# Seven products of halves for eight in the projections of an attention layer, and bv added to the residual

## The chip, the cores and the metric

The kernel runs on one core of a Trainium2 chip. The metric is device time in microseconds (us), the median of several runs; all runs told of here are in the fast state, that is, within 1.5% of the fastest run of the same kernel. In this kernel TensorE does the matrix products and writes them to PSUM, a memory in banks; VectorE, ScalarE and GpSimd do the rest between PSUM and SBUF, the memory of the operands, GpSimd on SBUF alone. The operand of a product that stays in TensorE while the other streams past is brought by an instruction of its own, the weight load. The granted clock is the share of TensorE's full speed that the profile shows. All data is float32.

In the profile's lines PE is TensorE, PEld its weight loads, DVE VectorE, ACT ScalarE, POOL GpSimd and SP SyncE, which starts transfers; L324 is a line of the kernel, `sc` are the scores, `pav` is the weighted sum, and `...` marks lines left out.

## The reference, cut to what matters

```python
# x: (128 batches, 128 nodes, 512 features); adj: (128, 128); H, HD = 8, 64
h = relu(layernorm(x))
A = einsum('od,bdn->bon', adj, h)                 # layer 0: W1 = W2 = adj, so that
x = x + max over n of relu(A + b)                 # its pairwise form comes down to this
h = relu(layernorm(x))                            # layer 1: adding a constant per row changes no layernorm
q, k, v = (h @ W + b for W, b in (Wq,bq), (Wk,bk), (Wv,bv))
scores = q k^T / sqrt(64), masked where adj == 0
x = x + softmax(scores) @ v                       # per head
```

The kernel therefore normalises once and uses the same h for both layers. Three 512 x 512 projections of 128 x 128 rows are most of the arithmetic.

## The kernel before

Batches go in 32 groups of four (G = 4, so T = 512 columns in a group). The loop is software-pipelined by hand: each group has four slots, one per batch. In a slot TensorE does a batch's scores, a piece of the next group's projections, and the batch's weighted sum (`finish`). Behind the loop the sums of the exponentials are tested (tile `ok`), and a general form of the kernel stands by for the case that one is out of range.

```python
def slice_q(g):                      # slice_k is the same with ScalarE; slice_v swaps the operands
    QT[g] = proj.tile([P, NC, T], F32, name="qT")
    for f in range(NC):
        pq = ps_mm.tile([P, 512], F32, name="mm")
        for c in range(NC):
            nc.tensor.matmul(pq, W["q"][:, c, f * P : (f + 1) * P], HT[g][:, c, :],
                             start=(c == 0), stop=(c == NC - 1))
        nc.vector.tensor_scalar(QT[g][:, f, :], pq, bq_sb[:, f : f + 1], HD ** -0.5,
                                op0=ALU.add, op1=ALU.mult)
# ... slice_h: four transposes and one adjacency product per batch, hT by ScalarE, maxima by VectorE
slices = (slice_h, slice_q, slice_k, slice_v)
# ... scores: 8 matmuls, two exps on ScalarE, two mask multiplications on VectorE
# ... finish: 8 matmuls (pav), reciprocal, o, y = X + c + o, store
for g in (0, 1):                     # the start
    for n in [norm(g, i) for i in range(G)]:
        norm_end(*n)
    if g == 0:
        for s in slices:
            s(0)
for g in range(NG):                  # the loop
    for i in range(G):
        # ...
        w = scores(g, i)
        n = norm(g + 2, i) if g + 2 < NG else None
        if g + 1 < NG:
            slices[i](g + 1)
        if n is not None:
            norm_end(*n)
        finish(g, i, w)
```

## Time and profile before

| | before |
|---|---|
| median | 1913.45 us (1913.2 to 1915.55, 4 runs) |
| TensorE busy | 1885.2 us, 7939 instructions |
| VectorE / ScalarE / GpSimd busy | 822.2 / 385.3 / 88.1 us |
| mean granted TensorE clock | 0.991 |
| one group in mid-run | 58.46 us |
| one projection of a group | 13.83 us |

The group's period is the distance of two starts of the q projection, 1011.92 us (shown in the prediction) and

```profile
1070.38 14.00 PE L272 MATMUL mm<-hT,wq_sb 128*128 128x512 f32 x32
```

The page is read from the chain that ended last and not from the busy shares: a busy TensorE is only the bound if the chain never leaves it.

### The profile page before, as it was taken

The page shows a single profiled execution, that of the slowest core. Times are in us where ns is not written, and L with a number is a line of the kernel's source. Part 1 is how long each engine was busy: PE and PEld are TensorE (multiplying, and loading weights), DVE is VectorE, ACT ScalarE, POOL GpSimd, SP SyncE. Part 2 cuts the span into 40 slices and gives each one's busy share as a digit, 9 for nine tenths or more (in the row PEclk, how much of TensorE's full clock was granted, in tenths as well). Part 3 has the DMA queues.
Part 4 walks back from the last instruction along what each step waited for, and adds up shares of the span by engine and source line. Part 5 has one row for each costly group of instructions (what it writes and reads, how often), then busy time and mean ns, then how long its engine had stood idle before and what let it go on. Part 6 is the DMA issues. An engine that isn't in the chain of part 4 may idle for free.

```text
span 1913.6 us, 19386 instructions
## 1 busy us (share of the span) xinstructions
PE 1885.2 (99%) x7939; PEld 1052.8 (55%) x7939; DVE 822.2 (43%) x1574; ACT 385.3 (20%) x641; POOL 88.1 (5%) x142
## 2 busy tenths in 40 slices
PE   7999999999999999999999999999999999999997
PEld 3455555555555555555555555555555555555555
DVE  2544344443445443444434454434444344544333
ACT  1222121221212221211212122212112121222110
POOL 1000000000000000000000000000000000000000
PEclk9999999999999999999999999999999999999996
DMA  4011011110111110111101111101111011110000
GB/s 161 11 39 39 17 39 45 39 45 12 44 39 45 39 39 17 40 44 39 45 11 45 39 44 39 39 17 41 42 39 45 11 45 39 45 39 17 17 20 31
DMA packets 37836, 71.87 MB, mean 38 GB/s; under 512 B 3249, under 2 KB 3377, under 8 KB 37745
## 3 DMA queue, kind: packets, MB, share of 16 engines
q1 hardware_dynamic: 35840, 67.12, 9.8%
q10 hardware_dynamic: 1728, 3.21, 0.5%
q8 instruction: 64, 1.05, 0.2%
q0 software_dynamic: 176, 0.27, 0.1%
q14 instruction: 28, 0.22, 0.0%
HBM read 37.03 MB, written 33.55 MB: 37 GB/s over the span
## 4 chain that ended last, share of the span: by engine, by line
PE 98%; DVE 1%; DMA 0%; ACT 0%; issue 0%; POOL 0%; SPq 0%; DVEq 0%
PE mm L272 23%; PE mm L298 23%; PE mm L286 23%; PE pav L332 12%; PE sc L315 7%; PE mm L263 6%; PE mm L256 3%; DMA xg<-in_x_dram 0%; DVE w L325 0%; DVE st L234 0%; DVE hn L240 0%; ACT w L323 0%; DVE y L344 0%; DVE o L340 0%; DVE mv L235 0%
## 5 line engine op out<-in xcount | busy, mean ns | idle before, releaser
L272 PE MATMUL mm<-hT,wq_sb 128*128 128x512 f32 x1024 | 448.0, 595 | 0.0
L298 PE MATMUL mm<-wv_sb,hT 128*128 128x512 f32 x1024 | 447.9, 595 | 0.0
L286 PE MATMUL mm<-hT,wk_sb 128*128 128x512 f32 x1024 | 447.9, 595 | 0.0
L323 ACT ACTIVATE w<-sc 128x512 f32<-128x512 f32 x256 | 138.9, 594 | 907.5 <-PE sc L315 907.5
L272 PEld LDWEIGHTS mm<-hT,wq_sb 128*128 128x128 f32 x1024 | 191.9, 190 | 234.0 <-issue 229.3
L286 PEld LDWEIGHTS mm<-hT,wk_sb 128*128 128x128 f32 x1024 | 192.0, 190 | 233.8 <-issue 222.9
L298 PEld LDWEIGHTS mm<-wv_sb,hT 128*128 128x128 f32 x1024 | 192.0, 190 | 233.8 <-issue 230.1
L332 PEld LDWEIGHTS pav<-v,w 128*128 128x128 f32 x2048 | 254.2, 195 | 66.7 <-issue 66.3
L332 PE MATMUL pav<-v,w 128*128 128x65 f32 x2048 | 249.0, 276 | 6.2 <-DVE w L325 6.1
L338 DVE RECIPROCAL RS<-pav 128x8 f32<-128x8 f32 x128 | 26.6, 208 | 480.6 <-PE pav L332 480.6
L302 DVE TENSOR_TENSOR v<-mm,bv_sb 128x512 f32<-128x512 f32 x128 | 88.5, 692 | 288.1 <-PE mm L298 288.1
L276 DVE TENSOR_SCALAR qT<-mm,bq_sb 128x512 f32<-128x512 f32 x128 | 96.1, 751 | 268.6 <-PE mm L272 268.6
L325 DVE TENSOR_TENSOR w<-w,live 128x512 f32<-128x512 f32 x256 | 165.6, 689 | 5.6 <-ACT w L323 4.5
L239 POOL TENSOR_TENSOR rstd<-ve,mhalf 128x1 f32<-128x1 f32 x128 | 84.4, 659 | 1720.2 <-DVE ve L237 1720.2
L290 ACT ACTIVATE kT<-mm,bk_sb 128x512 f32<-128x512 f32 x128 | 87.9, 687 | 359.8 <-PE mm L286 359.8
L315 PE MATMUL sc<-qT,kT 64*128 64x128 f32 x2048 | 151.5, 288 | 0.0
L263 PE MATMUL mm<-hn,adjT 128*128 128x512 f32 x256 | 133.5, 603 | 4.7 <-DVE adjT L225 4.3
L315 PEld LDWEIGHTS sc<-qT,kT 64*128 64x128 f32 x2048 | 126.7, 190 | 9.5 <-issue 0.8
L247 ACT ACTIVATE hn<-hn,rstd 128x512 f32<-128x512 f32 x128 | 92.1, 720 | 187.0 <-POOL rstd L239 187.0
L344 DVE SCALAR_TENSOR_TENSOR y<-xg,c,o 128x512 f32<-128x512 f32 x128 | 96.2, 752 | 4.5
L256 PEld LDWEIGHTS mm<-ident,hn 128*128 128x128 f32 x512 | 60.2, 143 | 65.9 <-issue 27.4
L234 DVE BATCH_NORM_STATS2 st<-xg 128x6 f32<-128x512 f32 x128 | 87.9, 687 | 7.3 <-DMA xg<-in_x_dram 7.3
(33 smaller groups left out, 487.5 us busy)
## 6 DMA issues: line engine op xcount, KB each, us to landing
xg<-in_x_dram SPq DMA_DIRECT2D x64, 512.0 KB, 4.6
out_dram<-y SPq DMA_DIRECT2D x128, 256.0 KB, 2.0
wq_sb<-in_L_gnn_Wq_dram ACTq DMA_DIRECT2D x1, 1024.0 KB, 11.0
wk_sb<-in_L_gnn_Wk_dram ACTq DMA_DIRECT2D x1, 1024.0 KB, 15.8
wv_sb<-in_L_gnn_Wv_dram ACTq DMA_DIRECT2D x1, 1024.0 KB, 19.7
bv_sb<-in_L_gnn_bv_dram POOLq DMA_DIRECT2D x1, 256.0 KB, 8.0
adj_sb<-in_adj_dram ACTq DMA_DIRECT2D x1, 64.0 KB, 2.4
b_sb<-in_L_gnn_b_dram POOLq DMA_DIRECT2D x1, 0.5 KB, 6.4
```

The lines of the kernel that those rows point to most:

```text
L247: nc.scalar.activation(HN[g][:, i, :], HN[g][:, i, :], AF.Copy, scale=rstd)
L256: nc.tensor.transpose(ph[:, c * D : (c + 1) * D], HN[g][:, i, c * P : (c + 1) * P], ident)
L263: nc.tensor.matmul(pa, adjT, HN[g][:, i, :], start=True, stop=True)
L272: nc.tensor.matmul(pq, W["q"][:, c, f * P : (f + 1) * P], HT[g][:, c, :], start=(c == 0), stop=(c == NC - 1),)
L276: nc.vector.tensor_scalar(QT[g][:, f, :], pq, bq_sb[:, f : f + 1], HD ** -0.5, op0=ALU.add, op1=ALU.mult,)
L286: nc.tensor.matmul(pk, W["k"][:, c, f * P : (f + 1) * P], HT[g][:, c, :], start=(c == 0), stop=(c == NC - 1),)
L298: nc.tensor.matmul(pv, HT[g][:, c, i * D : (i + 1) * D], W["v"][:, c, :], start=(c == 0), stop=(c == NC - 1),)
L315: nc.tensor.matmul(psc[:, j, f, :], KT[g][r, f, i * D : (i + 1) * D], QT[g][r, f, i * D : (i + 1) * D], start=True, stop=True,)
L323: nc.scalar.activation(w[:, j], psc[:, j], AF.Exp)
L325: nc.vector.tensor_tensor(w[:, j], w[:, j], live_h, op=ALU.mult)
L332: nc.tensor.matmul(pav[:, h // 4, (h % 4) * HE : (h % 4 + 1) * HE], w[:, h % 2, h // 2, :], V[g % 2][:, i, h, :], start=True, stop=True,)
L344: nc.vector.scalar_tensor_tensor(y, X[g][:, i, :], C[g][:, i : i + 1], o.rearrange("p k h d -> p (k h d)"), op0=ALU.add, op1=ALU.add,)
```

## The change

The intent is to spend fewer columns of TensorE's time on the projections, with one level of Strassen's method in the form of Winograd. Both operands are cut into halves along both axes; seven products of halves and some sums give what eight products gave. The sums of the weights are made once; those of hT, four per group, are VectorE's. Sums of products are made in two ways: a product is accumulated into a PSUM bank that holds another one, or VectorE adds a copy while it empties the bank. Since a bias would have to pass through these sums, bv is added to the residual X instead, on GpSimd; the weights of a softmax add up to one, so bv would pass through the weighted sum unchanged. The q scale moves into the exp. The transposes of a group move one slot ahead, as its sums are needed earlier. The tiles of `work`, the masked scores among them, get two buffers for three, and hn one for two. The cut shortens some lines; comments stand for the bodies of p1 to p7.

```diff
+            t1, t2, t3, t4 = (hs[:, k] for k in range(4))      # end of slice_h
+            nc.vector.tensor_sub(t1, b12, b11)
+            nc.vector.tensor_sub(t2, b22, t1)
+            nc.vector.tensor_sub(t3, b22, b12)
+            nc.vector.tensor_sub(t4, b21, t2)
+            def mm(self, bank, a, b, first=False):              # one product of halves
+                for r in range(2):
+                    for c in range(2):
+                        nc.tensor.matmul(
+                            bank[:, r, :], a[:, c, r * P : (r + 1) * P], b[:, c, :],
+                            start=first and r == 0 and c == 0, stop=r == 1 and c == 1, ...)
+            def p1(self): # bank a = a11 b11; ScalarE copies it out with each half's bias: pf[0], pf[1]
+            def p6(self): # bank b = s2 t2;   VectorE: u2 = b + pf[0]
+            def p2(self): # bank a += a12 b21; ScalarE: block (0, 0)
+            def p5(self): # bank c = s1 t1
+            def p7(self): # bank b += s3 t3;  VectorE: u3 = b + pf[1], block (1, 1) = c + u3
+            def p4(self): # bank b += a22 t4; VectorE: block (1, 0) = b + pf[1]
+            def p3(self): # bank c += s4 b22; VectorE: block (0, 1) = c + u2
+            return (                                            # the four slots
+                (q.p1, q.p6, q.p2, q.p5, q.p7, k.p1),
+                (q.p4, q.p3, k.p6, k.p2, k.p5, k.p7),
+                (v.p1, k.p4, k.p3, v.p6, v.p2, v.p5, v.p7),
+                (v.p4, v.p3),
+            )
+            nc.gpsimd.tensor_tensor(X[g][:, i, :], X[g][:, i, :], bv_sb, op=ALU.add)   # norm_end
-                    for s in slices:
-                        s(0)
+                slice_h(g)
+                if g == 0:
+                    weight_sums(nc.vector, "q")
+                    weight_sums(nc.gpsimd, "k")
+                    weight_sums(nc.gpsimd, "v")
+                    for part in products(0): ...
```

More of the change, by code (lines that the diff above doesn't have):

```diff
@@ L169, in tile_adj_preln_d2 @@
     T = G * D
+    HT2 = T // 2
     const = ctx.enter_context(tc.tile_pool(name="const", bufs=1))
@@ L173, in tile_adj_preln_d2 @@
     W = {n: const.tile([P, NC, N], F32, name=f"w{n}_sb") for n in "qkv"}
+    WS = {n: const.tile([P, 4, 2, N // 2], F32, name=f"s{n}_sb") for n in "qkv"}
     b0_sb = const.tile([P, 1], F32, name="b0_sb")
@@ L189, in fast @@
         proj = ctx.enter_context(tc.tile_pool(name="proj", bufs=2))
-        work = ctx.enter_context(tc.tile_pool(name="work", bufs=3))
+        work = ctx.enter_context(tc.tile_pool(name="work", bufs=2))
+        tmp = ctx.enter_context(tc.tile_pool(name="tmp", bufs=2))
         stat = ctx.enter_context(tc.tile_pool(name="stat", bufs=8))
@@ L194, in fast @@
         ps_av = ctx.enter_context(tc.tile_pool(name="ps_av", bufs=1, space=PSUM))
-        X, HN, HT, QT, KT, C, AMAX = {}, {}, {}, {}, {}, {}, {}
+        X, HN, HT, HB, QT, KT, C, AMAX, WA = {}, {}, {}, {}, {}, {}, {}, {}, {}
         def load(g):
@@ L230, in norm @@
             if i == 0:
-                HN[g] = proj.tile([P, G, N], F32, name="hn")
+                HN[g] = proj.tile([P, G, N], F32, name="hn", bufs=1)
             st = stat.tile([P, 6], F32, name="st")
@@ L265, in slice_h @@
             nc.vector.tensor_scalar(C[g], AMAX[g], b0_sb, 0.0, op0=ALU.add, op1=ALU.max)
-        def slice_q(g):
-            QT[g] = proj.tile([P, NC, T], F32, name="qT")
-            for f in range(NC):
-                pq = ps_mm.tile([P, 512], F32, name="mm")
-                for c in range(NC):
-                    nc.tensor.matmul(
-                        pq, W["q"][:, c, f * P : (f + 1) * P], HT[g][:, c, :],
-                        start=(c == 0), stop=(c == NC - 1),
-                    )
-                nc.vector.tensor_scalar(
-                    QT[g][:, f, :], pq, bq_sb[:, f : f + 1], HD ** -0.5,
-                    op0=ALU.add, op1=ALU.mult,
-                )
@@ L281, in slice_k @@
-        def slice_k(g):
-            KT[g] = proj.tile([P, NC, T], F32, name="kT")
-            for f in range(NC):
-                pk = ps_mm.tile([P, 512], F32, name="mm")
-                for c in range(NC):
-                    nc.tensor.matmul(
-                        pk, W["k"][:, c, f * P : (f + 1) * P], HT[g][:, c, :],
-                        start=(c == 0), stop=(c == NC - 1),
-                    )
-                nc.scalar.activation(
-                    KT[g][:, f, :], pk, AF.Identity, bias=bk_sb[:, f : f + 1]
-                )
@@ L294, in slice_v @@
-        def slice_v(g):
-            for i in range(G):
-                pv = ps_mm.tile([P, 512], F32, name="mm")
-                for c in range(NC):
-                    nc.tensor.matmul(
-                        pv, HT[g][:, c, i * D : (i + 1) * D], W["v"][:, c, :],
-                        start=(c == 0), stop=(c == NC - 1),
-                    )
-                nc.vector.tensor_add(
-                    V[g % 2][:, i, :, 0:HD], pv.rearrange("p (h d) -> p h d", h=H),
-                    bv_sb.rearrange("p (h d) -> p h d", h=H),
-                )
@@ L307, in fast @@
-        slices = (slice_h, slice_q, slice_k, slice_v)
+            t = HT[g]
+            b11, b12 = t[:, 0:2, 0:HT2], t[:, 0:2, HT2:T]
+            b21, b22 = t[:, 2:4, 0:HT2], t[:, 2:4, HT2:T]
+            hs = proj.tile([P, 4, 2, HT2], F32, name="hs", bufs=1)
+            t1, t2, t3, t4 = (hs[:, k] for k in range(4))
[3 more added lines that the diff above has]
+            nc.vector.tensor_sub(t4, b21, t2)
@@ new lines, in slice_h, with weight_sums @@
+            HB[g] = dict(b11=b11, b21=b21, b22=b22, t1=t1, t2=t2, t3=t3, t4=t4)
+        def weight_sums(eng, n):
+            w = W[n]
+            a11, a21 = w[:, 0:2, 0:HT2], w[:, 0:2, HT2:N]
+            a12, a22 = w[:, 2:4, 0:HT2], w[:, 2:4, HT2:N]
+            s1, s2, s3, s4 = (WS[n][:, k] for k in range(4))
+            eng.tensor_tensor(s1, a21, a22, op=ALU.add)
+            eng.tensor_tensor(s2, s1, a11, op=ALU.subtract)
+            eng.tensor_tensor(s3, a11, a21, op=ALU.subtract)
+            eng.tensor_tensor(s4, a12, s2, op=ALU.subtract)
+            WA[n] = dict(a11=a11, a12=a12, a22=a22, s1=s1, s2=s2, s3=s3, s4=s4)
@@ new lines, in fast, with __init__, dst, view @@
+        class Products:
+            def __init__(self, g, n):
+                self.g, self.n = g, n
+                if n == "q":
+                    QT[g] = proj.tile([P, NC, T], F32, name="qT")
+                elif n == "k":
+                    KT[g] = proj.tile([P, NC, T], F32, name="kT")
+            def dst(self, f, t):
+                if self.n == "v":
+                    return V[self.g % 2][:, 2 * t : 2 * t + 2, 4 * f : 4 * f + 4, 0:HD]
+                o = (QT if self.n == "q" else KT)[self.g]
+                return o[:, 2 * f : 2 * f + 2, t * HT2 : (t + 1) * HT2]
+            def view(self, ap):
+                return ap.rearrange("p r (h d) -> p r h d", d=HD) if self.n == "v" else ap
+            def mm(self, bank, a, b, first=False):
+                a, b = WA[self.n][a], HB[self.g][b]
+                if self.n == "v":
+                    a, b = b, a
+                for r in range(2):
+                    for c in range(2):
+                        nc.tensor.matmul(
+                            bank[:, r, :], a[:, c, r * P : (r + 1) * P], b[:, c, :],
+                            start=first and r == 0 and c == 0, stop=r == 1 and c == 1,
+                            skip_group_check=True,
+                        )
+            def bank(self):
+                return ps_mm.tile([P, 2, HT2], F32, name="mm")
+            def biased(self, out, bank, f):
+                if self.n == "v":
+                    nc.scalar.copy(out, self.view(bank))
+                    return
+                bias = bq_sb if self.n == "q" else bk_sb
+                for r in range(2):
+                    nc.scalar.activation(
+                        out[:, r], bank[:, r], AF.Identity,
+                        bias=bias[:, 2 * f + r : 2 * f + r + 1],
+                    )
+            def add(self, out, bank, more):
+                nc.vector.tensor_tensor(out, self.view(bank), self.view(more), op=ALU.add)
+            def p1(self):
+                self.a = self.bank()
+                self.mm(self.a, "a11", "b11", True)
+                self.pf = [tmp.tile([P, 2, HT2], F32, name="p1a")]
+                if self.n == "v":
+                    nc.scalar.copy(self.pf[0], self.a)
+                    self.pf.append(self.pf[0])
+                else:
+                    self.pf.append(tmp.tile([P, 2, HT2], F32, name="p1b"))
+                    for f in range(2):
+                        self.biased(self.pf[f], self.a, f)
+            def p6(self):
+                self.b = self.bank()
+                self.mm(self.b, "s2", "t2", True)
+                self.u2 = tmp.tile([P, 2, HT2], F32, name="u2")
+                nc.vector.tensor_tensor(self.u2, self.b, self.pf[0], op=ALU.add)
+            def p2(self):
+                self.mm(self.a, "a12", "b21")
+                self.biased(self.dst(0, 0), self.a, 0)
+            def p5(self):
+                self.c = self.bank()
+                self.mm(self.c, "s1", "t1", True)
+            def p7(self):
+                self.mm(self.b, "s3", "t3")
+                u3 = tmp.tile([P, 2, HT2], F32, name="u3")
+                nc.vector.tensor_tensor(u3, self.b, self.pf[1], op=ALU.add)
+                self.add(self.dst(1, 1), self.c, u3)
+            def p4(self):
+                self.mm(self.b, "a22", "t4")
+                self.add(self.dst(1, 0), self.b, self.pf[1])
+            def p3(self):
+                self.mm(self.c, "s4", "b22")
+                self.add(self.dst(0, 1), self.c, self.u2)
@@ L309, in scores, with products @@
+        def products(g):
+            q, k, v = (Products(g, n) for n in "qkv")
+            return (
[3 more added lines that the diff above has]
+                (v.p4, v.p3),
+            )
         def scores(g, i):
@@ L322, in scores @@
             for j in range(2):
-                nc.scalar.activation(w[:, j], psc[:, j], AF.Exp)
+                nc.scalar.activation(w[:, j], psc[:, j], AF.Exp, scale=HD ** -0.5)
             for j in range(2):
@@ L353, in fast @@
                     norm_end(*n)
+                slice_h(g)
                 if g == 0:
-                    for s in slices:
-                        s(0)
+                    weight_sums(nc.vector, "q")
+                    weight_sums(nc.gpsimd, "k")
+                    weight_sums(nc.gpsimd, "v")
+                    for part in products(0):
+                        for p in part:
+                            p()
             for g in range(NG):
+                parts = products(g + 1) if g + 1 < NG else ((),) * 4
                 for i in range(G):
@@ L362, in fast @@
                     n = norm(g + 2, i) if g + 2 < NG else None
-                    if g + 1 < NG:
-                        slices[i](g + 1)
+                    for p in parts[i]:
+                        p()
                     if n is not None:
                         norm_end(*n)
+                        if i == G - 1:
+                            slice_h(g + 2)
                     finish(g, i, w)
```

## The prediction

> **What bounds the kernel now.** I read the page's busy shares first, then the chain that ended last, the costliest groups, the waits of TensorE, and last a timeline of one group of four batches in mid-run.
>
> ```profile
> PE 1885.2 (99%) x7939; PEld 1052.8 (55%) x7939; DVE 822.2 (43%) x1574; ACT 385.3 (20%) x641; POOL 88.1 (5%) x142
> ...
> PE 98%; DVE 1%; DMA 0%; ACT 0%; issue 0%; POOL 0%; SPq 0%; DVEq 0%
> PE mm L272 23%; PE mm L298 23%; PE mm L286 23%; PE pav L332 12%; PE sc L315 7%; PE mm L263 6%; PE mm L256 3%; DMA xg<-in_x_dram 0%; DVE w L325 0%; DVE st L234 0%; DVE hn L240 0%; ACT w L323 0%; DVE y L344 0%; DVE o L340 0%; DVE mv L235 0%
> ```
>
> The chain never leaves TensorE (98%), and the three projections (L272 q, L286 k, L298 v) are 69% of the span. A busy row alone is not proof of full speed, so I looked for waits:
>
> ```profile
> PE pav L332 <- DVE w L325: 6.1, 4, 1.5
> PE mm L256 <- ACT hn L247: 4.9, 2, 2.7
> PE mm L224 <- POOL ident masks.py:199: 4.8, 1, 4.8
> PE mm L263 <- DVE adjT L225: 4.3, 1, 4.3
> ```
>
> All of them (us in total, times, longest) are one-time waits at the start and the end: some 25 us in 1913.6. In mid-run TensorE waits for nothing. What one projection really takes is read from the timeline (start, duration, engine, line):
>
> ```profile
> 1010.82 1.16 PE L315 MATMUL sc<-qT,kT 64*128 64x128 f32 x16
> ...
> 1011.92 14.00 PE L272 MATMUL mm<-hT,wq_sb 128*128 128x512 f32 x32
> ...
> 1012.45 0.19 PEld L272 LDWEIGHTS mm<-hT,wq_sb 128*128 128x128 f32 x1 [0.24 <-issue]
> ...
> 1012.88 0.19 PEld L272 LDWEIGHTS mm<-hT,wq_sb 128*128 128x128 f32 x1 [0.24 <-issue]
> ...
> 1025.75 1.90 PE L332 MATMUL pav<-v,w 128*128 128x65 f32 x16
> ...
> 1027.58 0.97 PEld L315 LDWEIGHTS sc<-qT,kT 64*128 64x128 f32 x16
> ```
>
> A weight load of 0.19 us comes every 0.43 us: one f32 matmul of the program is two instructions, each with its own load, 0.43 us apart. 32 of them are 13.83 us until pav starts, so the load lies wholly under the running matmul. pav (65 columns) needs 1.83 us for 16, 0.114 us each, and has the same 128-wide load: that is what a pair costs where the load is the longer part. sc takes 1.10 us.
>
> The evictions and sums that I price below are sized by these rows (busy us, mean ns | idle before, releaser):
>
> ```profile
> L325 DVE TENSOR_TENSOR w<-w,live 128x512 f32<-128x512 f32 x256 | 165.6, 689 | 5.6 <-ACT w L323 4.5
> L302 DVE TENSOR_TENSOR v<-mm,bv_sb 128x512 f32<-128x512 f32 x128 | 88.5, 692 | 288.1 <-PE mm L298 288.1
> L276 DVE TENSOR_SCALAR qT<-mm,bq_sb 128x512 f32<-128x512 f32 x128 | 96.1, 751 | 268.6 <-PE mm L272 268.6
> L290 ACT ACTIVATE kT<-mm,bk_sb 128x512 f32<-128x512 f32 x128 | 87.9, 687 | 359.8 <-PE mm L286 359.8
> ```
>
> **What the Trainium skill says.** "TensorE: Matmul & The Clock Gate", section "Back-to-back issue gap", gives N/2.4 + 2.5 ns for warm matmuls. With two passes of 512 columns per instruction that is 1024/2.4 + 2.5 = 429 ns; the trace's 0.43 us agrees, if an f32 instruction streams its columns twice. For 256 columns the same form is 512/2.4 + 2.5 = 216 ns, an estimate. The same page, section "The mechanism" of Part 3, says that a weight load overlaps a running matmul only in another row group. The trace differs: these are full 128-row loads and the gap stays at 0.43 us. "VectorE: DVE Perf Modes", section on the TRN2 errata, gives (N+151)/0.96 ns for an f32 tensor_tensor add, 691 ns at 512; the rows show 689 (SBUF) and 692 (PSUM), so I price each new add at 0.69. "GPSIMD Engine Reference", section "Key points", says that GpSimd shares its SBUF interfaces with VectorE, against instructions with two SBUF inputs among others, and that VectorE is about twice as fast elementwise: I take 1.4 us for a 512-element add there. Nothing in the trace before shows either of these two points.
>
> **The change part by part.** (1) TensorE, on the path. A projection of a group was 16 matmuls of 512 columns = 32 instructions; it becomes 7 products x 4 matmuls of 256 columns = 56 instructions. Per group and projection 32 x 0.429 = 13.73 us become 56 x 0.216 = 12.10. One product is 8 x 0.216 = 1.73 us. Over 3 projections and 32 groups: 96 x 1.63 = 157 us off. sc, pav, transposes and the adjacency product stay as they are.
>
> (2) VectorE, beside it. Removed: q and v evictions, 96.1 + 88.5 = 185 us. Added per group: 5 adds per projection and 4 sums of hT, 19 x 0.69 = 13.1 us, 420 us in all. 822 + 235 = 1057 us, some 59% of the new span: no bound by volume.
>
> (3) ScalarE, beside it, apart from one wait. The first product is copied out with two biases, four 256-wide activations for q and for k; the v copy is plain. I estimate a 256-wide one from the 687 ns row less 256 elements at about 0.9 ns (two exps of 512 take 1.08 us together in the timeline, so 512 elements add 0.49), 0.45 us, and four in a row 1.6 to 1.9 us. ScalarE gains about 110 us and stays under 30%.
>
> (4) The new waits. A bank is read and then accumulated into again, so a matmul may wait for a read. I went through one group with these durations, E being the end of the last adjacency product. pav 1.83, sc 1.09, then q's first product E+2.9 to 4.65, the sixth to 6.4, then the second, which writes the bank that ScalarE copies. The copies start 0.3 us after the product (the eviction at L276 trails its matmuls by that), E+4.95, and end at E+6.6 to 6.85: a wait of 0.2 to 0.5 us, once per group. k and v have other work between. Taken 0.4 with the restart: 32 x 0.4 = 13 us.
> The seventh q product wants its bank at E+10, after VectorE's u2. VectorE has before it the last maximum (E+0.2 to 0.9), c 1.15, four sums to 4.1, finish of the last batch to 5.85, masks 7.15, norm 8.65, u2 9.35: clear by 0.5 us. In the fourth slot the bank reuses by the transposes are clear by 0.2 to 0.5 us in the same count. So no wait there, but little room.
>
> (5) The start. The sixth q product now needs hT's sums and Wq's: six adds, 4.2 us, against 1.7 us of the first product, and GpSimd is adding bv and summing Wk and Wv at that time; 3 to 10 us, taken 6. The second group's normalisation now has to be done ahead of the first scores: 1.5 us of VectorE, 0.66 of GpSimd, 0.72 of ScalarE before a transpose can start, and the last pieces arrive at 1.5 us intervals: 5 us. The last v products of the first group follow each other with no scores between: 2 us. Together 13 us.
>
> (6) bv added to X on GpSimd, 128 x 1.4 = 180 us, beside everything; in mid-run it starts behind rstd, when VectorE's next work reads PSUM.
>
> Sum: 1913.5 - 157 + 13 + 13 = 1783 us.
>
> **The rivals.** (a) The weight load shows at 256 columns. 5376 loads that each added 0.1 us would cost 538 us and make it about 2320. The 0.43 us pace speaks against it, as does pav: 0.114 us per pair with the same load, so a load has room within 0.216. A few ns per instruction are possible; 5 ns are 27 us, 1810. (b) VectorE's order, not its volume, becomes the bound in the first slot: the chain of part (4) slips by 1 us (slower adds, GpSimd holding the shared interface), and the seventh product waits in each group: +16 to 32 us, 1800 to 1815. For it: the chain is nearly filled from E to E+9.35. Against: I found no two-SBUF-input add near a GpSimd add. (c) ScalarE's copies are slower than thought, or all three projections wait at their second product: 0.4 us three times a group would be +26 us more, 1809. Against: k and v have scores or other products in between. (d) The gain is hidden: transfers or another engine set the end. The page shows 10% DMA share or so and no chain but TensorE's, so I give it next to nothing.
>
> **Range and chances.** Streaming alone, without any wait, gives 1756; with (b) and (c) both, about 1840. I take 1762 to 1825. 2% faster is 1875 and would need 90 us more of waits than I count, 2.9 us per group: faster 0.94, same 0.04, slower 0.02.
>
> **What would show it.** Right: L324 has 5376 matmuls paced at 0.216 us, a product every 1.73 us, so the group's period falls from 58.4 us to about 53.5 plus 0.4; the waits list one per group at q's second product, behind ScalarE, near 0.4 us; VectorE near 1057 us busy. Wrong: a pace over 0.225 (rival a), 30 waits of the projection for u2 or for VectorE near a microsecond (rival b), or over 20 us lost before the second group.

## The result, and the profile after

| | before | after |
|---|---|---|
| median | 1913.45 us | 1776.35 us (1776.13 to 1778.04, 4 runs) |
| TensorE instructions | 7939 | 10243 |
| VectorE busy | 822.2 us | 1042.4 us |
| ScalarE busy | 385.3 us | 485.6 us |
| GpSimd busy | 88.1 us | 258.8 us |
| mean granted clock | 0.991 | 0.987 |
| one group in mid-run | 58.46 us | 53.80 us |

The ratio is 0.9283 (95% interval 0.9267 to 0.9299). A ratio is the mean time of one kernel's runs over that of the other's of the same rounds, so not quite the ratio of the medians quoted. The twelve runs of the experiments are correct.

The page of the changed kernel, its busy shares and the chain that ended last:

```profile
PE 1739.6 (98%) x10243; PEld 1492.6 (84%) x10243; DVE 1042.4 (59%) x1930; ACT 485.6 (27%) x961; POOL 258.8 (15%) x278
...
PE 98%; DVE 1%; DMA 0%; ACT 0%; issue 0%; POOL 0%; SPq 0%; DVEq 0%; ACTq 0%
```

The chain is still TensorE's. What fell is the time on it. The weight loads went from 55% to 84% of the span, since each instruction still brings its own load and there are more of them; that they are hidden is seen from the pace only. A group in mid-run (timeline: start, duration, engine, line, operation):

```profile
940.57 1.99 PE L324 MATMUL mm<-hT,wq_sb 128*128 128x256 f32 x8
...
942.40 1.89 PE L324 MATMUL mm<-hs,sq_sb 128*128 128x256 f32 x8
942.66 0.84 ACT L339 ACTIVATE p1a<-mm,bq_sb 128x256 f32<-128x256 f32 x2 [0.89 <-PE mm L324]
...
943.39 0.84 ACT L339 ACTIVATE p1b<-mm,bq_sb 128x256 f32<-128x256 f32 x2
...
944.28 1.99 PE L324 MATMUL mm<-hT,wq_sb 128*128 128x256 f32 x8
...
945.94 0.68 DVE L363 TENSOR_TENSOR u<-mm,p1a 128x512 f32<-128x512 f32 x1
...
946.11 3.62 PE L324 MATMUL mm<-hs,sq_sb 128*128 128x256 f32 x16
...
949.57 1.89 PE L324 MATMUL mm<-hT,wk_sb 128*128 128x256 f32 x8
...
994.36 1.99 PE L324 MATMUL mm<-hT,wq_sb 128*128 128x256 f32 x8
```

The starts are what is read here, since the modelled ends overlap. The next group's q begins at 994.36, and the one before began at 886.77: 53.80 us each. From 946.11 to 949.57 two products are 3.46 us: 1.73 each, 0.216 us per instruction. The sixth product of q (942.40) is followed after 1.88 us: the second one was held for 0.15 us until ScalarE's four copies were done (943.39 + 0.84 = 944.23). It then took 1.83 us to the next, 0.10 more than a product that follows another one without a stop. Its first weight load starts together with it, at 944.28, while that of the sixth product starts 0.22 us ahead of it (942.18). The first product behind the scores, 940.57 to 942.40, takes 1.83 us as well. u2 ended at 946.62, and the seventh product, which needs that bank, was due at 947.84: 1.2 us of room. The waits of TensorE (us in total, times, longest):

```profile
PE mm L324 <- DVE sq_sb L293: 8.7, 1, 8.7
PE mm L265 <- ACT hn L255: 6.4, 2, 3.3
PE pav L420 <- DVE w L413: 6.1, 4, 1.5
...
PE mm L324 <- DVE u L376: 0.8, 1, 0.8
PE mm L324 <- ACT p1b L339: 0.3, 1, 0.3
```

The one that comes in every group is nearly invisible in this list, as it is shorter than the modelled tail of the product before it. The list of the weight loads has it:

```profile
PEld mm L324 <- ACT p1b L339: 12.5, 31, 0.7
```

31 times, 0.4 us each: the time in which the load sat idle, not the time that was lost. So the list of waits says where and how often, but what it costs has to be tried (below). The remaining waits are at the start and the end.

### The profile page after: what moved, and what is told of

Same layout as the page of the kernel before. It is cut to its first block, busy times and chain, and to the rows that moved or that the text cites. A ratio compares the mean times of both kernels' runs of the same rounds, so it can differ in the third digit from the quotient of the medians.

```text
span 1776.2 us, 24850 instructions
## 1 busy us (share of the span) xinstructions
PE 1739.6 (98%) x10243; PEld 1492.6 (84%) x10243; DVE 1042.4 (59%) x1930; ACT 485.6 (27%) x961; POOL 258.8 (15%) x278
## 3 DMA queue, kind: packets, MB, share of 16 engines
q1 hardware_dynamic: 35840, 67.12, 10.5%
## 4 chain that ended last, share of the span: by engine, by line
PE 98%; DVE 1%; DMA 0%; ACT 0%; issue 0%; POOL 0%; SPq 0%; DVEq 0%; ACTq 0%
PE mm L324 67%; PE pav L420 13%; PE sc L403 8%; PE mm L272 6%; PE mm L265 3%; DMA xg<-in_x_dram 0%; DVE w L413 0%; DVE st L242 0%; ACT w L411 0%; DVE sq_sb L292 0%; DVE hs L283 0%; DVE hs L284 0%; DVE sq_sb L293 0%; DVE hs L282 0%; DVE y L432 0%
## 5 line engine op out<-in xcount | busy, mean ns | idle before, releaser
L324 PE MATMUL mm<-hs,sq_sb 128*128 128x256 f32 x768 | 178.1, 382 | 8.7 <-DVE sq_sb L293 8.7
L324 PE MATMUL mm<-hs,sk_sb 128*128 128x256 f32 x768 | 176.2, 379 | 0.0
L324 PE MATMUL mm<-sv_sb,hs 128*128 128x256 f32 x768 | 176.2, 379 | 0.0
L324 PEld LDWEIGHTS mm<-hs,sq_sb 128*128 128x128 f32 x768 | 146.9, 191 | 29.2 <-DVE sq_sb L293 9.1
L324 PEld LDWEIGHTS mm<-sv_sb,hs 128*128 128x128 f32 x768 | 145.9, 190 | 19.8
L324 PEld LDWEIGHTS mm<-hs,sk_sb 128*128 128x128 f32 x768 | 145.9, 190 | 19.8
L256 POOL TENSOR_TENSOR xg<-xg,bv_sb 128x512 f32<-128x512 f32 x128 | 162.1, 1269 | 0.0
L324 PE MATMUL mm<-hT,wq_sb 128*128 128x256 f32 x512 | 127.7, 392 | 0.3 <-ACT p1b L339 0.3
L324 PE MATMUL mm<-wv_sb,hT 128*128 128x256 f32 x512 | 124.2, 385 | 0.0
L324 PE MATMUL mm<-hT,wk_sb 128*128 128x256 f32 x512 | 120.9, 379 | 0.0
## 6 DMA issues: line engine op xcount, KB each, us to landing
wq_sb<-in_L_gnn_Wq_dram ACTq DMA_DIRECT2D x1, 1024.0 KB, 10.5
```

Of the source, the lines that this page charges most:

```text
L256: nc.gpsimd.tensor_tensor(X[g][:, i, :], X[g][:, i, :], bv_sb, op=ALU.add)
L324: nc.tensor.matmul(bank[:, r, :], a[:, c, r * P : (r + 1) * P], b[:, c, :], start=first and r == 0 and c == 0, stop=r == 1 and c == 1, ski ...
```

## The experiments

**Are short matmuls as good as long ones?** `e1_halves` is the kernel before with all eight products, each matmul cut in two.

```diff
-            nc.tensor.matmul(pq, W["q"][...], HT[g][:, c, :], ...)
+            for u in range(0, 512, 256):
+                nc.tensor.matmul(pq[:, u : u + 256], W["q"][...], HT[g][:, c, u : u + 256], ...)   # k, v alike
```

> The kernel before with every projection matmul of 512 columns cut into two of 256: all eight products, no Strassen sums. Theory (a 256-wide f32 instruction costs 0.216 us, its weight load hidden): 3072 more instructions at 2.5 ns, so +8 us, 1921 us. Rival (the changed kernel's gain is partly lost to short matmuls, the load shows): each of the 6144 instructions over 0.22 us, +30 us or more.

Measured: 1924.21 us, ratio 1.0058 (1.0043 to 1.0074), 11 us more. One projection in its timeline:

```profile
1015.89 14.08 PE L275 MATMUL mm<-hT,wq_sb 128*128 128x256 f32 x64
1029.81 1.90 PE L343 MATMUL pav<-v,w 128*128 128x65 f32 x16
```

64 instructions in 13.92 us, against 13.83 for the 32 long ones: +0.09 us. The group's period is 58.70 us (1015.89 to 1074.59), 0.24 more, 32 times: 8 us as expected. In the profiled executions the last matmul comes 7.6 us later (1918.16 against 1910.55), and 2.8 us more lie behind it (5.8 against 3.0 us), where no engine's work is shown; their cause is open. The rival, a load that shows at 256 columns, falls. Without the eighth product saved, the short form would have been a small loss.

**Where does the load become the bound?** `e9_quarters` cuts q's matmuls, and only q's, into 128 columns.

```diff
-CW = 512
+CW = 128        # q alone; k and v stay at 512
```

> The kernel before with q's matmuls alone cut into four of 128 columns. It asks where the weight load becomes the bound, which a second level of halving would meet. Theory (a pair of load and matmul can't go faster than pav's 0.114 us): 128 x 0.114 = 14.6 us per group in place of 13.8, +25 us, 1938 us. Rival (streaming alone counts, 256/2.4 + 2.5 = 0.109 us): +6 us, 1919 us.

Measured: 1934.07 us, ratio 1.0106 (1.0089 to 1.0123), 21 us more.

```profile
1021.90 14.56 PE L275 MATMUL mm<-hT,wq_sb 128*128 128x128 f32 x128
1036.30 1.90 PE L343 MATMUL pav<-v,w 128*128 128x65 f32 x16
```

14.40 us for 128 instructions, 0.1125 each. That lies between the two theories; the rival's 0.109 us is worked out with the form that the prediction took from the skill. But some 0.11 us of the 14.40 are the first load behind the scores: in the first group, where that load runs ahead (19.92 for 20.34), the same 128 instructions take 14.29 us (20.34 to 34.63), 0.1116 each, midway between 0.109 and 0.114. So pav's pace is not a floor for a pair, and that the load sets the pace here is not shown. In the total, 32 x 0.57 = 18 us are in the projections; 2.7 us lie behind the last matmul, as in e1. An estimate from the pace: a second level of halving would need 49 products of 2 instructions at 0.112 = 11.0 us against 56 x 0.216 = 12.1 per projection and group, some 110 us in all, for a great many more sums on VectorE. I did not run that.

**Does each projection bring its share?** `e10_v_plain` takes v back to eight products.

```diff
-                (v.p1, k.p4, k.p3, v.p6, v.p2, v.p5, v.p7),
-                (v.p4, v.p3),
+                (k.p4, k.p3, lambda: plain_v(g, (0, 1, 2))),
+                (lambda: plain_v(g, (3,)),),
```

> The changed kernel with v back to eight products of 512 columns, the rest unchanged: VectorE has 35 us less to do and TensorE streams an eighth more for v. Theory (each projection's seven products save 1.63 us per group, by streaming alone): 32 x 1.63 = +52 us, 1828 us. Rival (the gain comes from the new order of the slots or from k and q alone): less than +40 us.

Measured: 1827.34 us, ratio 0.955 (0.9534 to 0.9566), 51 us above the changed kernel. Two starts of q:

```profile
1023.02 1.99 PE L324 MATMUL mm<-hT,wq_sb 128*128 128x256 f32 x8
...
1078.46 1.99 PE L324 MATMUL mm<-hT,wq_sb 128*128 128x256 f32 x8
```

The group's period is 55.44 us, 1.64 more than 53.80, as the streaming sum says. VectorE had less to do in this run and the time rose, and the order of the slots was kept, so neither of the two gave v's share of the gain. q and k were not taken back one by one; for them the pace of the products and the period stand.

**The part with bv.** `e2_bv_alone` makes only this part of the change.

```diff
-                nc.vector.tensor_add(V[...], pv..., bv_sb...)
+                nc.vector.tensor_copy(V[...], pv...)
             nc.scalar.activation(HN[g][:, i, :], HN[g][:, i, :], AF.Copy, scale=rstd)
+            nc.gpsimd.tensor_tensor(X[g][:, i, :], X[g][:, i, :], bv_sb, op=ALU.add)
```

> The kernel before with only the bv part of the change: GpSimd adds bv to X, V is copied out without a bias. Theory (TensorE alone sets the time): 1913 us within 3 us, GpSimd busy up by about 162 us. Rival (moving work off VectorE is part of the gain, or GpSimd disturbs VectorE): a change of over 5 us either way.

Measured: 1920.1 us, ratio 1.0037 (1.0022 to 1.0052): 7 us slower, so my theory missed and the rival had it. The slots in mid-run are those of before (8.2 and 16.75 us between starts of the scores); 5.9 us of the loss lie ahead of 83 us. The q projection of the second group starts at 82.48 us, against 76.56 before. At that place, the second group's four adds ran without a break while VectorE came to the first batch's mask multiplications:

```profile
69.46 5.83 POOL L248 TENSOR_TENSOR xg<-xg,bv_sb 128x512 f32<-128x512 f32 x4
...
70.76 3.41 DVE L325 TENSOR_TENSOR w<-w,live 128x512 f32<-128x512 f32 x2 [1.68 <-ACT w L323]
...
76.29 1.12 PE L264 MATMUL mm<-hn,adjT 128*128 128x512 f32 x2 [2.50 <-DVE amax L265]
```

Two multiplications took 3.41 us, where the kernel before has them at 1.29, and TensorE waited 2.5 us in place of 0.4 for the maxima behind them to release a PSUM bank. TensorE then ran at a granted clock of 0.54 (77 to 84 us). From the first scores (62.68, before 61.18) to the second group's q, 4.4 us are lost, and the slow clock takes 0.9 more in that projection (14.74 us in place of 13.83). Another 1.5 us are lost already at the first group's q (21.30 against 19.80), where the adds met no mask multiplications: there TensorE's clock came up later. That differs from run to run without any add, too: from the first adjacency product to q it takes 6.5 us in the kernel before, 7.2 in e1 and e9, 7.8 here.

`e11_bv_later` issues the second group's adds behind the second batch's scores. It also moves the first group's four, from its normalisation to the end of its projections, which its expectation does not say, so it doesn't tell the two apart.

```diff
+            if g > 1:                             # in norm_end
+                add_bv(g, i)
+                    for i in range(G):            # behind the first group's projections
+                        add_bv(0, i)
                     w = scores(g, i)
+                    if g == 0 and i == 1:
+                        for j in range(G):
+                            add_bv(1, j)
```

> The bv part alone again, but the second group's four bv adds are issued later, behind the second batch's scores, so that they don't meet the first batch's mask multiplications. With the adds where the change has them those two multiplications took 3.4 us in place of 1.3 and the kernel was 7 us slower, all of it before 83 us. Theory (GpSimd's burst of four adds holds VectorE's two-input work at the start, and bv costs nothing in mid-run): the multiplications are back at 1.3 us, 1916 us or less. Rival (the 7 us have another cause): 1920 us.

Measured: 1913.0 us, ratio 0.9997 (0.998 to 1.0014). The line of the multiplications:

```profile
69.12 1.29 DVE L329 TENSOR_TENSOR w<-w,live 128x512 f32<-128x512 f32 x2 [1.67 <-ACT w L327]
```

The second group's q starts at 76.42. So in this kernel bv on the residual costs nothing that shows; the burst of GpSimd adds beside the mask multiplications, which have two inputs in SBUF, does. The burst now meets the second batch's multiplications (2.35 us for the two), where TensorE has a projection to do and nobody waits.

**The wait in each group.** `e3_second_later` exchanges two products of q.

```diff
-                (q.p1, q.p6, q.p2, q.p5, q.p7, k.p1),
+                (q.p1, q.p6, q.p5, q.p2, q.p7, k.p1),
```

> The changed kernel with q's fifth product ahead of its second, so that ScalarE's four copies have 1.7 us more. Theory (q's second product waits 0.16 us per group for ScalarE's copies and for nothing else): 31 x 0.16 = 5 us less, 1771 us, and the product before it takes 1.73 in place of 1.89 us in the timeline. Rival (the 0.16 us is a restart cost of reusing a bank, or it moves to the next wait): no change.

Measured: 1766.96 us, ratio 0.9236 (0.9223 to 0.9249), 9.4 us below the changed kernel where I expected 5. The group's period is 53.54 us (936.10 to 989.64), 0.26 less. The sixth and fifth product now run into each other:

```profile
937.93 3.62 PE L324 MATMUL mm<-hs,sq_sb 128*128 128x256 f32 x16
941.39 1.89 PE L324 MATMUL mm<-hT,wq_sb 128*128 128x256 f32 x8
```

A stop of 0.15 us had cost 0.26, since the product behind the stop took 0.10 us more. 31 x 0.26 is 8 us; in the start 0.3 us more are gained. The last us is the clock at the end: the first wait of the last group is the same 1.52 us, but the weighted sum behind it takes 2.46 us here (1735.50 to 1737.96) and 3.62 in the changed kernel (1744.15 to 1747.77). Nothing in this edit explains that, and the same piece takes 2.8 us in the kernel before, so about 1 us of a difference between two of these runs can be luck.

**The start.** In the changed kernel the sixth product of the first group waited 8.7 us for Wq's sums. Two of VectorE's six adds ahead of it, and one of GpSimd's beside them:

```profile
22.14 1.64 DVE L282 TENSOR_TENSOR hs<-hT,hs 128x512 f32<-128x512 f32 x1
...
23.19 1.70 POOL L292 TENSOR_TENSOR sv_sb<-wv_sb 128x512 f32<-128x512 f32 x1
23.70 1.74 DVE L283 TENSOR_TENSOR hs<-hT 128x512 f32<-128x512 f32 x1
...
30.50 3.78 PE L324 MATMUL mm<-hs,sq_sb 128*128 128x256 f32 x8 [8.67 <-DVE sq_sb L293]
34.07 2.21 PE L324 MATMUL mm<-hT,wq_sb 128*128 128x256 f32 x8
```

Both engines' adds are stretched, VectorE's from 0.69 to 1.7 us and GpSimd's from 1.27 to 1.7, and they alternate. `e4_sums_off_gpsimd` gives the sums of Wk and Wv to VectorE, after the products that it then has to wait for anyway.

```diff
-                    weight_sums(nc.gpsimd, "k")
-                    weight_sums(nc.gpsimd, "v")
-                    for part in products(0):
+                    for j, part in enumerate(products(0)):
                         for p in part:
                             p()
+                        if j < 2:
+                            weight_sums(nc.vector, "kv"[j])
```

> The changed kernel with the sums of Wk and Wv on VectorE, after the first and second part of the first group's products. Theory (VectorE's two-input adds at the start took 1.6 to 1.75 us because GpSimd's adds held the shared interface): those adds return to 0.69 us, the wait of 8.7 us for Wq's sums falls to about 4 us, and the slow clock behind it goes: 1770 us or a little less. Rival (VectorE's adds were slow for landing weights or another reason): adds stay at 1.6 us and the time at 1776.

Measured: 1770.68 us, ratio 0.9256 (0.9243 to 0.9269), 5.7 us less.

```profile
21.36 0.69 DVE L282 TENSOR_TENSOR hs<-hT,hs 128x512 f32<-128x512 f32 x1
...
24.64 3.78 PE L326 MATMUL mm<-hs,sq_sb 128*128 128x256 f32 x8 [3.17 <-DVE sq_sb L296]
28.22 3.03 PE L326 MATMUL mm<-hT,wq_sb 128*128 128x256 f32 x8
```

The adds are back at 0.69 us and the wait is 3.2. I had expected the slow clock to go, and it did not: the sixth product and the second together take 6.45 us here (24.64 to 31.09), 5.61 in the changed kernel (30.50 to 36.11), in place of 3.46. The granted clock was 0.54 in that stretch. How long the slow stretch lasts does not follow the wait: with the start of the changed kernel unaltered, in e10, the two products took 5.20 us behind a wait of 8.5.

**Is there room on VectorE?** `e7_one_more` and `e8_four_more` put one and four idle passes of 512 elements between the normalisation and u2 in the first slot of each group.

```diff
                     n = norm(g + 2, i) if g + 2 < NG else None
+                    if i == 0 and n is not None:
+                        for _ in range(1):        # e8: range(4)
+                            junk = stat.tile([P, 6], F32, name="junk")
+                            nc.vector.bn_stats(junk, X[g][:, i, :])
```

> The changed kernel with one more VectorE pass over 512 elements (a statistics instruction whose result nobody reads, 0.72 us with its gap) in the first slot of each group, between the normalisation and u2. In the changed kernel u2 ended 1.2 us before q's seventh product was to start. Theory (VectorE has 1.2 us of room there and its 59% do not bind): no change, 1776 within 2 us. Rival (the chain through VectorE is what the mid-run waits hang on): +0.7 us per group, +22 us.

> The same with four of them, 2.9 us. Theory: the room of 1.2 us is used up and 1.7 us per group shows as a wait of q's seventh product for u2, 30 groups: +50 us, 1826 us, though VectorE is only about 61% busy. Rival (VectorE's volume is what counts and it has 40% to spare): no change.

Measured: 1777.4 us with one (ratio 0.9289, 0.9273 to 0.9304: the changed kernel's), 1806.02 us with four (0.9439, 0.9423 to 0.9455). The waits with four:

```profile
PE mm L324 <- DVE u L363: 22.0, 30, 1.1
```

The direction is the theory's, the size is not: 30 us in place of 50. In the trace the four passes delayed u2 by 2.05 us and not by 2.9 (7.43 us after q's first product in place of 5.37): they run 0.6 us apart, and some of the pause that u2 had anyway is used. Less the room of 1.2 us that is 0.9 us of wait (due at 964.40, started at 965.28) and 0.1 behind it, and the period grew by 0.98 (54.78 us). VectorE had 38% of the span free and TensorE waited for it all the same: what counts is the place in its queue.

**Putting it together.** `e5_start_reordered` takes the product order of e3, has all weight sums on VectorE with Wq's ahead of the transposes, spreads the second group's normalisation through the first group's products, and adds the first two groups' bv later.

```diff
+            weight_sums(nc.vector, "q")
+            slice_h(0)
+            for j, part in enumerate(products(0)):   # ... with norm_end(*norm(1, j)) after each part,
+                ...                                  #     the sums of Wk, Wv after parts 0 and 1,
+            slice_h(1)                               #     add_bv(0, i) after part 2
+            for i in range(G):
+                add_bv(1, i)
```

> The changed kernel with q's second product late, all weight sums on VectorE with Wq's ahead of the transposes, the second group's normalisation spread through the first group's products, and the first two groups' bv added later. Theory (what the change lost against its streaming sum lies in the start and in that one wait): -9 us for the product order, -6 for the sums, -5 for the rest of the wait for Wq's sums and its slow clock, -5 for the second group's normalisation: about 1751 us. Rival (waits only move): 1761 us or more.

Measured: 1757.17 us, ratio 0.9186 (0.917 to 0.9201), 6 us more than expected. Part of the gain was given back: Wq's sums now stood ahead of the copy of the transposed adjacency, and the first adjacency product waited 4.9 us for it, 1.8 more than in the changed kernel. `e6_end_overlapped` adds this to it:

```diff
+                    w = scores(g, i) if wn is None else wn
+                    if g == NG - 1:
+                        wn = scores(g, i + 1) if i + 1 < G else None
```

> The same, and in the last group the next batch's scores go ahead of the weighted sum of the batch before. In the changed kernel each of these four batches took 7.3 us at half the granted clock, behind a wait of 1.5 us for the masks. Theory: the batches take some 3 us each: 15 us less, about 1736 us. Rival (VectorE's 2.9 us per batch and slow clock keep them at 5 us or more): -8 us or less.

Measured: 1744.58 us, ratio 0.912 (0.9105 to 0.9136), 12.6 us less. One of the last batches, first of the changed kernel and then of this one:

```profile
1751.37 3.76 PE L420 MATMUL pav<-v,w 128*128 128x65 f32 x16 [1.52 <-DVE w L413]
...
1758.65 3.76 PE L420 MATMUL pav<-v,w 128*128 128x65 f32 x16 [1.51 <-DVE w L413]
```

```profile
1724.42 2.00 PE L426 MATMUL pav<-v,w 128*128 128x65 f32 x16
...
1727.54 1.97 PE L426 MATMUL pav<-v,w 128*128 128x65 f32 x16
```

7.28 us per batch became 3.12. Only 1.5 us of the old ones were the wait; pav took 3.7 us for its 1.83, as the granted clock was 0.56 from 1741 to 1774 us. The kernel before has the same end (0.56 from 1880 to 1911 us), so this gain is not one of the seven products. `e12_best` moves the transpose of the adjacency matrix ahead of the third batch's normalisation and splits Wq's sums around the maxima.

```diff
+            for n in [norm(0, i) for i in range(2)]:
+                norm_end(*n)
+            adjacency()
+            for n in [norm(0, i) for i in range(2, G)]:
+                norm_end(*n)
```

> The version with the start reordered and the end overlapped, with the adjacency transpose ahead of the third batch's normalisation and Wq's sums split around the maxima: in the run before, the first adjacency product waited 4.9 us for the transpose's copy, behind those sums. Theory: 3 to 5 us less than 1744.6, about 1740 us. Rival (input still sets the start): no change.

Measured: 1739.03 us (1738.67 to 1739.48), ratio 0.9089 (0.9074 to 0.9104). The wait for the transposed adjacency is gone from the list, and the first group's q starts at 17.04 us in place of 20.83. This is the fastest version, 37 us below the changed kernel and 174 below the one before.

## Why the prediction was right

The measured 1776.35 us lies 7 us below the predicted 1783, inside 1762 to 1825. The sum was 157 off, 13 for the wait in each group and 13 for the start; measured were 137 off in all.

1. **Streaming, 157 us.** Right. 0.216 us per instruction and 1.73 per product are in the timeline, the period fell by 4.66 us (4.89 by the sum, less the wait of 0.26), and taking back v cost its 51 us. The two rivals here, a load that shows (e1) and a gain from anything but the streaming (e10), fell.
2. **The wait at q's second product.** The mechanism was right and the term was too large: 0.4 us per group predicted, 0.26 lost by e3, 8 us in place of 13. The count itself said 0.2 to 0.5, and I took 0.4 "with the restart"; the trace has 0.15 of stop and 0.10 of restart. The stop was smaller for two reasons: ScalarE's four copies take 1.57 us from first to last, a little under my 1.6 to 1.9, and q's first product takes 1.83 us behind the scores where I had 1.75, so the second was due 0.1 us later. k and v did not wait at their second products (the starts at 957.77, 959.49 and 961.22 us are 1.73 apart, those at 972.87, 974.60 and 976.33 as well), so rival (c) fell. I had read the pace of 0.429 from a formula; the 13.83 us of 32 instructions are 0.10 more than that, the first load, which does not lie under anything.
3. **The start, 13 us.** The total was about right by errors that cancelled. I had 6 us for Wq's sums; the wait was 8.7, and the slow clock behind it took 2.2 more (5.61 less 3.46). This is the term that was mis-sized most: 10.9 us for 6. I had named the shared interface and put too little on it, and had not thought of the clock at all. I had 5 us for the second group's normalisation; between its neighbours, that group's transposes took 10.5 us in place of 5.2, but the kernel before had a like loss in the same place (11.4 us from the end of its first scores to the first weighted sum). The change only moved it, and I forgot to take the old one off. For the last v products I had 2 us; they waited 0.8. The second group's q starts at 79.87 us, in the kernel before at 76.56; there a weighted sum and scores (2.9 us) stand ahead of it, and the streaming sum takes off 4.9, so the changed kernel had lost 11 us. That the start came within 2 us is luck: the term for Wq's sums was 5 us too small and the one for the normalisation some 6 too large.
4. **VectorE and bv.** 1057 us predicted, 1042.4 measured; a bv add took 1.27 us, predicted 1.4. That they would lie beside TensorE in mid-run held. The room at the seventh product was 1.2 us and not the 0.5 that I counted, and it is a real limit (e8). That GpSimd's bv would meet no two-input work of VectorE was right in mid-run. At the start it was GpSimd's weight sums that met VectorE's, as part (5) had feared; the bv adds there (12.74 to 17.67 and 75.12 to 80.07 us) stood beside VectorE's maxima, which read PSUM, but for 0.06 us. So the loss at the masks that e2 shows belongs to the old order of the slots and is no part of the changed kernel's. Rival (b) did not come true: no wait for u2 is listed in mid-run.

The sum of the parts closes: 157 less 8 less 11 is 138, and 137 were measured. Of the 7 us by which the prediction was too high, 5 are the wait in each group and 2 the start.

## What to carry to other kernels

Where TensorE streams without a stop, as in mid-run here, fewer columns were worth just their time, and matmuls of half the width cost next to nothing (0.09 us in 13.8) as their loads stayed under the stream: measure the pace, not the busy share. A method that turns matmuls into sums must be laid out by the queue of the engine that sums, for what it costs is where in its queue a needed sum stands and not how much it has to do. Look at the start and the end with their own eyes: a wait there was followed by a stretch at about half the clock (2 to 3 us lost behind the waits for Wq's sums), and reordering them brought 28 us with no arithmetic changed, on top of the 9 from one exchange of products.

## What the Trainium skill lacked or had wrong

- "TensorE: Matmul & The Clock Gate", Part 3, section "The mechanism", says in one line that weight loads overlap a running matmul only where the row group differs, and a few lines above also allows it for a background weight buffer. Here full 128-row loads are hidden, which the first would not allow: 64 instructions with 64 loads take 13.92 us (e1). The prediction had told only the first.
- The same page, section "Back-to-back issue gap", has no figure for f32. The runs show two instructions for each f32 matmul of the program, 0.43 us each at 512 columns, 0.216 at 256 and 0.112 at 128. Down to 256 columns that is its formula with twice the columns; at 128 it is 0.002 us more.
- The same page, Part 1, puts the slow clock behind an idle window of some 3.4 us; it speaks of shorter idle times as well, but gives no length for them. In the last group a single wait of 1.5 us was followed by a weighted sum in 3.62 us in place of 1.83, and waits of 1.5 us in every 7.3 kept the granted clock at 0.56.
- "GPSIMD Engine Reference", section "Key points", names the contention with two-input VectorE work and no size. Other pages of the skill describe how one engine blocks the other, so only the sizes are new: VectorE's adds of 512 elements go from 0.69 to 1.7 us and GpSimd's from 1.27 to 1.7 while both run, and two mask multiplications from 1.29 to 3.41.
- No page has the price of a short stop: 0.15 us of wait cost 0.26 us per group (e3), as the first weight load behind it is not ahead of its product.
